# The seam between the LSTM layer and the attention layer: last outputs moved into layer 1's first two steps, its weight loads and first transposes moved ahead

## The chip, the cores and the metric

One core of one Trainium2 chip runs the whole kernel, in fp32. The metric is the device time in microseconds of one execution; the median of three runs stands for a kernel. Beside these runs there is one profiled execution, from which every duration of a single instruction in this text comes.

## The reference

The input x has 128 x 64 tokens of 256 features (8192 tokens), and passes four layers, each of the form x = x + f(relu(layernorm(x))). What matters here is the end of layer 0 and the start of layer 1:

```python
# layer 0: two graph convolutions, then LSTMs over windows of 1 to 4 time steps
h = relu(einsum('ts,bsh->bth', adj, x @ Wg0 + bg0))
h = relu(einsum('ts,bsh->bth', adj, h @ Wg1 + bg1))
for p in range(1, 5):
    nw = T // p
    wins = h[:, :nw * p].reshape(B * nw, p, H)
    last = lstm_last(Wih[p-1], Whh[p-1], bih[p-1], bhh[p-1], wins)
    h = h.at[:, arange(nw) * p + (p - 1)].set(last)
x = x + h
# layer 1: edge attention over 512 edges of a 64-node graph, 4 heads
h  = relu(layernorm(x))
Xq, Xv = h @ W_lin.T, h @ W_val.T
e  = einsum('behd,hd->beh', leaky_relu(Xq[:, src] + Xq[:, dst]), a) + log(A0[src, dst])
x  = x + (segment_softmax(e, src) applied to Xv[:, dst]) @ W_out.T
```

Layer 2 is a graph convolution with batch norms and weights W1 and W2; layer 3 is a dense graph attention.

## The kernel before, in words

**Tiling.** Tokens come in 16 chunks of 512 (NCH), each held as 4 x 128 tokens by 256 features; four chunks make a group (NGR = 4 groups). Matrix products want the features on the partitions, layer norms want the tokens there, so TensorE transposes between the two forms: `transpose_features` (transposes L153, ACT copy L156) turns a normed chunk to features-first; `add_transposed` (transposes L167, DVE add L172) turns an LSTM result back and adds it to the residual.

**End of layer 0.** The LSTMs run as products (L643) of TensorE with Strassen-like quarter sums, and gates: ACT activations L671, DVE additions L697 and L702, the cell update L720 and L721, tanh L724, and the hidden state `hT` L737 (these line numbers are those of the profile of before). Products land in a PSUM pool in which `bank()` has two buffers. A list of slots orders the products; for each group, two calls of `group_out(g, c)` are hung behind the slots. Such a call takes two chunks: for each, 8 transposes, 2 DVE adds into the residual tile `xres` (4 buffers, loaded from x by SP in `fetch_x`, L764), and one store of the new x into `xa[n]` on POOL's queue (L776). The calls of the last group come after the last slot, when there are no products left.

**Start of layer 1.** The first two chunks of `xa` are loaded and normed among the last LSTM slots (`x_first`, `first_norms1`). Then the code allocates layer 1's pools (its PSUM pool gives `bank()` four buffers), issues on SP the loads of the weights `wlv` and `wout`, of layer 2's `w1T` and `w2T`, of six vectors, and of chunks 2 and 3 (`load_x1`, tiles `xin`); it transposes chunk 0, projects two tiles of 128 tokens, and enters the loop over pairs of tiles, `edges(q)`, q = 0 to 31. A step of it gathers queries to the edges (L964), lets ACT copy the result (L970) and DVE apply the leaky relu (L971), scores (L980), projects the next pair (`project`, L948, with copies L954 and L955), and norms chunks ahead: statistics on DVE (L87, L88), roots on POOL (L99 to L102), scaling on ACT (L109). `w1T` gets four POOL instructions of quarter sums (L136). The residual tiles `xo` of layer 1 are loaded from `xa` by SP (L1121).

**What sets the order.** Each engine runs its instructions in order. A planner places them by its own priorities; `late(...)` marks an instruction that keeps its place in program order. A tile pool makes the first writer of a buffer wait for the last users of its memory, and pools opened later reuse the memory of pools that were closed, so a load can wait for layer 0's last readers of that place.

Of the kernel before, what the change touches and what calls it, by code (L numbers as in the profile page):

```python
# [9 lines left out]
F32 = mybir.dt.float32  # L10
# [20 lines left out]
def gnn_stack_kernel(ctx: ExitStack, tc: tile.TileContext, a: dict, out: bass.AP):  # L31
# [373 lines left out]
            yield  # L405


    with ExitStack() as l0:
        w0 = l0.enter_context(tc.tile_pool(name="w0", bufs=1))
        wsp = l0.enter_context(tc.tile_pool(name="wsp", bufs=1))  # L410

        hTs0 = [w0.tile([P, 2, 2, UNIT], F32, tag=f"hT{k}", name=f"hT{k}") for k in range(NGR // 2)]
# [169 lines left out]
        hop = lpool("hop2", 2)  # L582
        cp = lpool("cp", 2)
        gp = lpool("gp", 8)
        xres = lpool("xres", 4)

        class Step:

# [172 lines left out]

        def fetch_x(n):
            xt = xres.tile([P, 4, D], F32, tag="xres", name="xres")
            nc.sync.dma_start(out=xt, in_=token_tiles(a["x"], n))  # L764
            return xt

        residual = {}
# [41 lines left out]
        steps[0].prepare()  # L809
        for slot in range(len(tasks) + 2):  # L810
            new = tasks[slot] if slot < len(tasks) else None
            if new:
                step = steps[new[0]]
                one = step.gate(new[1])
                next(one)
            if len(flight) > 1:
                old = flight.pop(0)
                next(old[1], None)
                next(flight[-1][1])
            elif flight and not new:  # L820
                old = flight.pop(0)
                next(old[1], None)
            else:
                old = None
                if flight:
                    next(flight[-1][1])
            if new:
                next(one)
                flight.append((new, one))
                at, k = new[0], new[2]  # L830
                while outs and outs[0][0] <= slot:
                    group_out(*outs.pop(0)[1:])

                new_half = at + 1 < len(steps) and at and steps[at + 1].w == 1 < step.w
                if k == len(step.gates) - (1 if new_half else 2) and at + 1 < len(steps):
                    steps[at + 1].prepare()
                if step.w == MAX_SKIP and step.t == 2 and k < 2:
                    for u in range(2):
                        n = 4 * step.g + 2 * u + k
                        later.append((slot, "x", n))  # L840
            while later and later[0][0] <= slot:
                _, kind, n = later.pop(0)
                residual[n] = fetch_x(n)
            next(norm_steps, None)
            while later_weights and later_weights[0][0] <= slot:
                _, ph = later_weights.pop(0)
                weights["ih", ph] = Weights("ih", phases[ph])
            if old:
                (at, q, k), step = old[0], steps[old[0][0]]
                if k == len(step.gates) - 1:  # L850
                    if at + 1 == len(steps) or steps[at + 1].phase != step.phase:
                        phase_over(step.phase)
                    if step.phase == len(phases) - 1 and step.t == 1 and step.g == NGR - 1:

                        t_ = wsp.tile([P, 2, 4, 2, P], F32, tag="wih", name="x_first", bufs=2)
                        flat = t_.rearrange("p k q j m -> p k (q j m)")
                        norms1 = {}
                        for n in range(2):
                            xt = flat[:, n, :].rearrange("p (i d) -> p i d", i=4)
                            nc.sync.dma_start(out=xt, in_=token_tiles(xa[n]))  # L860
                            norms1[n] = Norm(xt)
                        norm_steps = first_norms1(norms1)
                    if step.w == MAX_SKIP and step.t == MAX_SKIP - 1:
                        outs += [(slot + 1, step.g, 0), (slot + 2, step.g, 1)]
        for _ in norm_steps:
            pass
        for _, g, c in outs:
            group_out(g, c)
    psums["banks"] = None
    w12 = ctx.enter_context(tc.tile_pool(name="w12", bufs=1, side="right"))  # L870
    xin1 = l01.enter_context(tc.tile_pool(name="xin1", bufs=2, side="right"))

    def load_x1(n, chunks=xa):
        xt = xin1.tile([P, 4, D], F32, tag="xin1", name="xin1")
        nc.sync.dma_start(out=xt, in_=token_tiles(chunks[n]))
        return xt


    with ExitStack() as l1:
# [5 lines left out]
            return l1.enter_context(tc.tile_pool(name=name, bufs=bufs, reuse_waits="tile"))  # L885


        t1 = pool("t1", 2)
        lrp = pool("lrp", 6)
        t3 = pool("t3", 4)  # L890
        w1 = pool("w1", 1)
        vp = pool("vp", 3)
        KEPT = 4
        vk = pool("vk", KEPT)
        yp = pool("yp", 2)
        xo = pool("xo", 4)
        e1 = pool("e1", 1)
        attp = pool("attp", 3)
        attc = pool("attc", 3)
        wlv = w1.tile([P, 2, 2 * D], F32, tag="wlv", name="wlv")  # L900
        nc.sync.dma_start(out=wlv[:, :, :D], in_=a["W_linT"])
        nc.sync.dma_start(out=wlv[:, :, D:], in_=a["W_valT"])
        wout = w1.tile([P, 2, D], F32, tag="wout", name="wout")
        nc.sync.dma_start(out=wout, in_=a["W_outT"])


        w1T = w12.tile([P, 2, 512], F32, tag="w1T", name="w1T")
        nc.sync.dma_start(out=w1T, in_=a["W1T"])
        w2T = w12.tile([P, 4, D], F32, tag="w2T", name="w2T")
        nc.sync.dma_start(out=w2T, in_=a["W2T"])  # L910
        w1S = w12.tile([P, 3, 2, P], F32, tag="w1S", name="w1S")
        w1Q = quarter_sums(w1T.rearrange("p k (q j m) -> p k q j m", q=2, j=2), w1S)
        x_rs = w12.tile([P, NCH, 4], F32, tag="x_rs", name="x_rs")
        x_nm = w12.tile([P, NCH, 4], F32, tag="x_nm", name="x_nm")
        vec = {}
        for name, width in (("b1", 4), ("g1", 4), ("be1", 4), ("b2", 2), ("g2", 2), ("be2", 2)):
            vec[name] = w12.tile([P, width], F32, tag=name, name=name)
            nc.sync.dma_start(out=vec[name], in_=a[name])
        hTs, queries, values, scores, waiting = {}, {}, {}, {}, []

        def sums1(m, tiles):

# [17 lines left out]
        def project(it):  # L940

            n, i = it // 4, it % 4
            if i == 0:
                kept = n >= NCH - KEPT
                values[n] = (vk if kept else vp).tile([P, 4, D], F32, tag="xv", name="xv")
            p = bank()
            for k in range(2):
                ins = nc.tensor.matmul(  # L948
                    p, hTs[n][:, k, i * P : (i + 1) * P], wlv[:, k, :], start=k == 0, stop=k == 1
                )  # L950
                if k == 0:
                    late(ins)
            xq = queries[it] = t3.tile([P, D], F32, tag="xq", name="xq")
            nc.scalar.copy(xq, p[:, :D])  # L954
            (nc.vector.tensor_copy if i % 2 else nc.scalar.copy)(values[n][:, i, :], p[:, D:])  # L955
            if i == 3 and n < NCH - KEPT:
                nc.gpsimd.dma_start(out=xv_mem[n], in_=values.pop(n))
# [147 lines left out]
        def fetch(n):  # L1105
# [4 lines left out]
                xv = vp.tile([P, 4, D], F32, tag="xv", name="xv_in")  # L1110
                nc.sync.dma_start(out=xv, in_=xv_mem[n])
            if n < NCH - 3:
                xt = xo.tile([P, 4, D], F32, tag="xo", name="xo")
            else:

                if n < NCH - 1:
                    t = t1.tile([P, 2, CHUNK], F32, tag="hT1", name="xo_last")
                else:
                    t = w1.tile([P, 2, 2 * D], F32, tag="wlv", name="xo_last")
                xt = t.rearrange("p c t -> p (c t)").rearrange("p (i d) -> p i d", d=D)  # L1120
# [3 lines left out]
        def turn_attention(n):  # L1124

            g, m = n // 4, n % 4
            att = attc.tile([P, 2, 8, T], F32, tag="att", name="att")
            for o in range(2):
                late(
                    (nc.vector.tensor_copy if o else nc.scalar.copy)(  # L1130
# [52 lines left out]
        def sums(n, xt, keep=False):  # L1183
# [3 lines left out]
            for i in range(4):  # L1187
                nc.vector.bn_stats(st[:, i, :], xt[:, i, :])
                nc.vector.bn_aggr(mv[:, i, :], st[:, i, :])
            rs, nm = x_rs[:, n, :], x_nm[:, n, :]  # L1190
            ins = nc.gpsimd.tensor_scalar(rs, mv[:, :, 1], 1e-5, None, ALU.add)
            if keep:
                late(ins)
# [63 lines left out]
        def edges(q):  # L1257
# [5 lines left out]
            for it in tiles:  # L1263
                if it + 2 < NT:
                    project(it + 2)
            if not odd:
                turn1(n + 1)
                sums1(n + 2, (2, 3))
# [15 lines left out]
                    turn_attention(k)  # L1284

        coming1 = {n: load_x1(n) for n in (2, 3)}
        hTs[0] = t1.tile([P, 2, CHUNK], F32, tag="hT1", name="hT1")
        for ip in range(2):
            transpose_features(norms1[0].h, hTs[0], ip)
        sums1(2, (0, 1))  # L1290
        for it in range(2):
            project(it)
        for q in range(NT // 2):
            edges(q)
            last_one = q == NT // 2 - 1

            for _ in range(4 if last_one else 0):
# [8 lines left out]
        def scale_x(n, xt, keep=late):  # L1306

            h2[n] = hpool.tile([P, 4, D], F32, tag="h", name="h")
            for i in range(4):
# [2 lines left out]
                        h2[n][:, i, :],  # L1312
                        xt[:, i, :],
                        AF.Relu,
                        bias=x_nm[:, n, i : i + 1],
                        scale=x_rs[:, n, i : i + 1],
                    )
                )

# [12 lines left out]
        while unnormed:  # L1332
            sums(*unnormed.pop(0))
    l01.close()


    with ExitStack() as l2:
# [623 lines left out]
```

## Time and profile before

| | us |
|---|---|
| median of 3 runs | 2087.89 |
| lowest and highest run | 2086.41, 2092.74 |
| profiled execution | 2079.25 |
| span of the profile | 2077.5 |
| TensorE busy (PE) | 2013.7 (97%) |
| DVE, ACT, POOL busy | 1359.9, 1180.2, 315.7 |
| granted TensorE clock, mean | 0.994 |

PE is TensorE's matmul stream (transposes too), PEld its weight loads, which overlap it. L-numbers are lines of the kernel. An engine's own time within a stretch is read from the windows view, what it waited for from the waits view, the order of one engine's work from its timeline. In a timeline a row is the start, the time from the first to the last of the instructions put together, the engine, line, operation and count, and in brackets the idle time ahead of it and who ended it. SPq and POOLq are the queues on which those engines issue transfers.

### The profile page before, as it was taken

Reading aid. Unit: us, or ns where it says so; the run is one execution under the profiler, and the core shown is the slowest. Engines: PE = TensorE matmul, PEld = TensorE weight load, DVE = VectorE, ACT = ScalarE, POOL = GpSimd, SP = SyncE. Lnnn points to the kernel's source line nnn. Section 1 sums busy time; section 2 is a strip of 40 time slices with the busy share of each in tenths; the row PEclk is TensorE's granted clock in tenths of the full one; section 3 lists DMA queues with packets and bytes.
Section 4 is the critical chain, followed back from the end, with each engine's and each line's share of the span. In section 5 each row is a group of like instructions: output and inputs, shape, how many; then the busy total and the mean of one; then the engine's idle time right before and its main releaser. Section 6 shows DMA issues by size and latency. Waiting matters only on the chain.

```text
span 2077.5 us, 25503 instructions
## 1 busy us (share of the span) xinstructions
PE 2013.7 (97%) x9444; PEld 1350.0 (65%) x9444; DVE 1359.9 (65%) x2508; ACT 1180.2 (57%) x2226; POOL 315.7 (15%) x422
## 2 busy tenths in 40 slices
PE   8999999999999999999999998999999999999998
PEld 6777478866688845886667886333334765434786
DVE  7664666564665567567446555677777767786776
ACT  4344766554555467566456563666675456592444
POOL 3000010110100021002001001223233420000563
PEclk9999999999999999999999999999999999999999
DMA  8421000100100160001001006213234851022012
GB/s 276 134 96 52 0 21 1 41 0 1 41 1 1 64 220 21 1 1 41 1 0 41 1 1 205 74 51 98 76 92 123 253 185 59 0 71 91 31 62 71
DMA packets 94460, 135.06 MB, mean 65 GB/s; under 512 B 6400, under 2 KB 82048, under 8 KB 92160
## 3 DMA queue, kind: packets, MB, share of 16 engines
q1 hardware_dynamic: 87616, 109.11, 16.0%
q0 software_dynamic: 6112, 24.12, 4.0%
q8 instruction: 74, 1.21, 0.2%
q14 instruction: 50, 0.41, 0.1%
q10 hardware_dynamic: 608, 0.20, 0.0%
HBM read 87.28 MB, written 46.14 MB: 64 GB/s over the span
## 4 chain that ended last, share of the span: by engine, by line
PE 87%; DVE 6%; ACT 3%; DMA 2%; issue 1%; POOL 1%; ACTq 0%; POOLq 0%; DVEq 0%; SPq 0%
PE pa L643 25%; PE bank L50 13%; PE pc L643 13%; PE pb L643 6%; PE pair L964 6%; PE bank L948 5%; PE pa L1396 5%; PE bank L980 3%; PE bank L1169 3%; PE pc L1396 2%; PE pb L1396 1%; PE pair L50 1%; ACT gate L671 1%; PE pair L1148 1%; PE bank L167 1%
## 5 line engine op out<-in xcount | busy, mean ns | idle before, releaser
L643 PE MATMUL pa<-xop,sih 128*128 128x256 f32 (+2 forms) x1056 | 344.3, 418 | 10.1 <-DVE gate L697 6.4
L671 ACT ACTIVATE gate<-gate,bias 128x256 f32<-128x256 f32 (+2 forms) x368 | 247.1, 678 | 173.5 <-DVE gate L687 91.2
L643 PEld LDWEIGHTS pa<-xop,sih 128*128 128x128 f32 x1056 | 198.3, 190 | 86.4 <-issue 22.8
L643 PE MATMUL pc<-xop,wih 128*128 128x256 f32 (+2 forms) x736 | 251.1, 423 | 0.0
L687 DVE TENSOR_TENSOR gate<-pb,gate 128x256 f32<-128x256 f32 (+2 forms) x184 | 87.6, 476 | 225.7 <-PE pb L643 154.1
L643 PE MATMUL pa<-lstm_h,shh 128*128 128x256 f32 (+1 forms) x672 | 212.7, 398 | 0.0
L971 DVE SCALAR_TENSOR_TENSOR lr<-lr 128x1024 f32<-128x1024 f32 x128 | 150.5, 1218 | 55.6 <-ACT lr L970 55.6
L643 PEld LDWEIGHTS pc<-xop,wih 128*128 128x128 f32 x736 | 139.8, 190 | 51.2 <-issue 23.0
L702 DVE TENSOR_TENSOR gate<-pc,gate 128x256 f32<-128x256 f32 (+2 forms) x184 | 87.6, 476 | 119.7 <-PE pc L643 119.4
L970 ACT COPY lr<-pair 128x1024 f32<-128x1024 f32 x128 | 123.1, 1014 | 45.1 <-PE pair L964 45.1
L643 PEld LDWEIGHTS pa<-lstm_h,shh 128*128 128x128 f32 x672 | 127.7, 190 | 30.2
L643 PE MATMUL pc<-lstm_h,whh 128*128 128x256 f32 (+1 forms) x448 | 141.8, 398 | 0.0
L686 ACT COPY gate<-pa 128x256 f32<-128x256 f32 (+2 forms) x184 | 76.0, 413 | 96.7 <-PE pa L643 96.4
L964 PE MATMUL pair<-sd_hot,xq 64*128 64x512 f32 x512 | 127.6, 616 | 2.4 <-ACT lr L970 2.3
L948 PE MATMUL bank<-wlv,hT 128*128 128x512 f32 x256 | 118.1, 604 | 0.2 <-ACT hT L156 0.2
L697 DVE TENSOR_TENSOR gate<-pa,gate 128x256 f32<-128x256 f32 (+2 forms) x184 | 87.5, 475 | 44.0 <-PE pa L643 43.4
L691 ACT COPY gate<-pa 128x256 f32<-128x256 f32 (+2 forms) x184 | 75.4, 410 | 59.0 <-PE pa L643 57.7
L671 ACT ACTIVATE gate<-pa,bias 128x256 f32<-128x256 f32 (+2 forms) x184 | 94.0, 511 | 26.1 <-PE pa L643 24.4
L434 POOL TENSOR_TENSOR sih<-wih 128x512 f32<-128x512 f32 x8 | 11.8, 1474 | 624.8 <-DMA wih<-in_WihT 295.9
L643 PE MATMUL pa<-xop,wih 128*128 128x256 f32 (+1 forms) x320 | 101.4, 398 | 2.7 <-ACT xop L624 2.7
L643 PE MATMUL pb<-xop,wih 128*128 128x256 f32 (+1 forms) x320 | 100.3, 398 | 1.6 <-DVE gate L687 1.6
L643 PEld LDWEIGHTS pc<-lstm_h,whh 128*128 128x128 f32 x448 | 85.1, 190 | 20.1
(338 smaller groups left out, 3814.8 us busy)
## 6 DMA issues: line engine op xcount, KB each, us to landing
field<-sd_hot SPq DMA_DIRECT2D x8, 1152.0 KB, 11.4
wih<-in_WihT SPq DMA_DIRECT2D x8, 1024.0 KB, 5.0
xres<-in_x SPq DMA_DIRECT2D x16, 512.0 KB, 4.5
xa<-xres POOLq DMA_DIRECT2D x16, 512.0 KB, 5.3
xin<-xb SPq DMA_DIRECT2D x16, 512.0 KB, 3.9
h<-xb SPq DMA_DIRECT2D x16, 512.0 KB, 3.9
xin<-in_x SPq DMA_DIRECT2D x15, 512.0 KB, 5.5
out_x<-h SPq DMA_DIRECT2D x15, 512.0 KB, 2.9
```

What stands on the lines that cost most here:

```text
L50: nc.tensor.matmul(o, lhsT, rhs, start=start, stop=stop)
L643: ins = nc.tensor.matmul(p[:, : self.N], weights[kind, self.phase](k, q), x[k], start=first_ and kind == "ih", stop=kind == "hh" or not se ...
L671: nc.scalar.activation(out, in_, AF.Tanh if q == 2 else AF.Sigmoid, bias=bias[:, self.w - 1, 2 * q + j : 2 * q + j + 1],)
L686: nc.scalar.copy(blk[0, 0], pa[:, :N])
L687: nc.vector.tensor_tensor(blk[0, 0], pb[:, :N], blk[0, 0], ALU.add)
L697: nc.vector.tensor_tensor(blk[1, 1], pa[:, :N], blk[1, 1], ALU.add)
L702: nc.vector.tensor_tensor(blk[1, 0], pc[:, :N], blk[1, 0], ALU.add)
L948: ins = nc.tensor.matmul(p, hTs[n][:, k, i * P : (i + 1) * P], wlv[:, k, :], start=k == 0, stop=k == 1)
L964: ins = nc.tensor.matmul(p[:, par, :], queries[it][r, c * P : (c + 1) * P], sd_hot[r, :], start=True, stop=True)
L970: nc.scalar.copy(lr, p)
L971: nc.vector.scalar_tensor_tensor(lr, lr, 0.2, lr, ALU.mult, ALU.max)
L1396: ins = nc.tensor.matmul(p, lhs[k], x[k], start=first_, stop=last_one, skip_group_check=True)
```

## The change

1. `group_out` for the last group is no longer called after the LSTM slots. Its two calls are made in `edges(0)` and `edges(1)`, behind the projections. The pool of `xres` and that of the hidden states live until q = 1 is done, on the other side of the memory.
2. `wlv` and `wout` are loaded ahead of the last four loads of x, which move from the slots to layer 1's start and are kept in program order by `late`.
3. The transposes of chunk 0 go to the first slot behind the last LSTM product in the program, into a gate buffer (`first_hT`), in program order.
4. The loads of layer 2's weights and vectors, the quarter sums of `w1T`, and the pools `vk`, `xo` and `attc` come after q = 1 (`layer2_weights`). Other pools of layer 1 change their order of allocation; `xin1` moves to the left side.

```diff
+    l0out = ExitStack()
+    w0 = l0out.enter_context(tc.tile_pool(name="w0", bufs=1, side="right"))
     with ExitStack() as l0:
-        w0 = l0.enter_context(tc.tile_pool(name="w0", bufs=1))
...
-        xres = lpool("xres", 4)
+        xres = l0out.enter_context(
+            tc.tile_pool(name="xres", bufs=4, side="right", reuse_waits="tile")
+        )
...
         def fetch_x(n):
             xt = xres.tile([P, 4, D], F32, tag="xres", name="xres")
-            nc.sync.dma_start(out=xt, in_=token_tiles(a["x"], n))
+            ins = nc.sync.dma_start(out=xt, in_=token_tiles(a["x"], n))
+            if n >= NCH - NCH // 4:
+                late(ins)
             return xt
...
         for slot in range(len(tasks) + 2):
             new = tasks[slot] if slot < len(tasks) else None
+            if slot == len(tasks):
+                for _ in norm_steps:
+                    pass
+                first_hT = gp.tile([P, 4 * NMAX], F32, tag="gate", name="hT1_first")
+                first_hT = first_hT[:, : 2 * CHUNK].rearrange("p (c t) -> p c t", c=2)
+                for ip in range(2):
+                    transpose_features(norms1[0].h, first_hT, ip, late)
...
-                if step.w == MAX_SKIP and step.t == 2 and k < 2:
+                if step.w == MAX_SKIP and step.t == 2 and k < 2 and step.g < NGR - 1:
                     for u in range(2):
                         n = 4 * step.g + 2 * u + k
                         later.append((slot, "x", n))
...
-        for _ in norm_steps:
-            pass
-        for _, g, c in outs:
-            group_out(g, c)
+        last_outs = [(g, c) for _, g, c in outs]
     psums["banks"] = None
-    w12 = ctx.enter_context(tc.tile_pool(name="w12", bufs=1, side="right"))
-    xin1 = l01.enter_context(tc.tile_pool(name="xin1", bufs=2, side="right"))
...
         nc.sync.dma_start(out=wlv[:, :, :D], in_=a["W_linT"])
         nc.sync.dma_start(out=wlv[:, :, D:], in_=a["W_valT"])
         wout = w1.tile([P, 2, D], F32, tag="wout", name="wout")
         nc.sync.dma_start(out=wout, in_=a["W_outT"])
-        w1T = w12.tile([P, 2, 512], F32, tag="w1T", name="w1T")
-        nc.sync.dma_start(out=w1T, in_=a["W1T"])
...
+        for g, c in last_outs:
+            for u in range(2):
+                n = 4 * g + 2 * u + c
+                residual[n] = fetch_x(n)
...
+        def layer2_weights():
+            w12 = ctx.enter_context(tc.tile_pool(name="w12", bufs=1, side="right"))
+            w1T = w12.tile([P, 2, 512], F32, tag="w1T", name="w1T")
+            nc.sync.dma_start(out=w1T, in_=a["W1T"])
...
+            w1S = w12.tile([P, 3, 2, P], F32, tag="w1S", name="w1S")
+            w1Q = quarter_sums(w1T.rearrange("p k (q j m) -> p k q j m", q=2, j=2), w1S)
...
             for it in tiles:
                 if it + 2 < NT:
                     project(it + 2)
+            if last_outs:
+                group_out(*last_outs.pop(0))
             if not odd:
                 turn1(n + 1)
                 sums1(n + 2, (2, 3))
...
         coming1 = {n: load_x1(n) for n in (2, 3)}
-        hTs[0] = t1.tile([P, 2, CHUNK], F32, tag="hT1", name="hT1")
-        for ip in range(2):
-            transpose_features(norms1[0].h, hTs[0], ip)
+        hTs[0] = first_hT
         sums1(2, (0, 1))
         for it in range(2):
             project(it)
         for q in range(NT // 2):
             edges(q)
+            if q == 1:
+                l0out.close()
+                layer2_weights()
+                for name, bufs in (("vk", KEPT), ("xo", 4), ("attc", 3)):
+                    later_pools[name] = pool(name, bufs)
```

More of the change, by code (lines that the diff above doesn't have):

```diff
@@ L864, in gnn_stack_kernel @@
                         outs += [(slot + 1, step.g, 0), (slot + 2, step.g, 1)]
-        for _ in norm_steps:
-            pass
-        for _, g, c in outs:
-            group_out(g, c)
+        last_outs = [(g, c) for _, g, c in outs]
     psums["banks"] = None
-    w12 = ctx.enter_context(tc.tile_pool(name="w12", bufs=1, side="right"))
-    xin1 = l01.enter_context(tc.tile_pool(name="xin1", bufs=2, side="right"))
[L873 to L876, printed above, removed]
     with ExitStack() as l1:
@@ L885, in pool, with load_x1 @@
             return l1.enter_context(tc.tile_pool(name=name, bufs=bufs, reuse_waits="tile"))
+        KEPT = 4
+        w1 = pool("w1", 1)
         t1 = pool("t1", 2)
+        t3 = pool("t3", 4)
+        vp = pool("vp", 3)
         lrp = pool("lrp", 6)
[L890 to L894, printed above, removed]
+        xin1 = pool("xin1", 2)
         yp = pool("yp", 2)
-        xo = pool("xo", 4)
         e1 = pool("e1", 1)
         attp = pool("attp", 3)
-        attc = pool("attc", 3)
+        later_pools = {}
+        def load_x1(n, chunks=xa):
+            xt = xin1.tile([P, 4, D], F32, tag="xin1", name="xin1")
+            nc.sync.dma_start(out=xt, in_=token_tiles(chunks[n]))
+            return xt
         wlv = w1.tile([P, 2, 2 * D], F32, tag="wlv", name="wlv")
@@ L904, in gnn_stack_kernel @@
         nc.sync.dma_start(out=wout, in_=a["W_outT"])
-        w1T = w12.tile([P, 2, 512], F32, tag="w1T", name="w1T")
[L908 to L918, printed above, removed]
-        hTs, queries, values, scores, waiting = {}, {}, {}, {}, []
+        for g, c in last_outs:
+            for u in range(2):
+                n = 4 * g + 2 * u + c
+                residual[n] = fetch_x(n)
+        hTs, queries, values, scores, waiting = {}, {}, {}, {}, []
+        vec, w12t = {}, {}
+        def layer2_weights():
+            w12 = ctx.enter_context(tc.tile_pool(name="w12", bufs=1, side="right"))
+            w1T = w12.tile([P, 2, 512], F32, tag="w1T", name="w1T")
+            nc.sync.dma_start(out=w1T, in_=a["W1T"])
+            w2T = w12.tile([P, 4, D], F32, tag="w2T", name="w2T")
+            nc.sync.dma_start(out=w2T, in_=a["W2T"])
+            w1S = w12.tile([P, 3, 2, P], F32, tag="w1S", name="w1S")
+            w1Q = quarter_sums(w1T.rearrange("p k (q j m) -> p k q j m", q=2, j=2), w1S)
+            x_rs = w12.tile([P, NCH, 4], F32, tag="x_rs", name="x_rs")
+            x_nm = w12.tile([P, NCH, 4], F32, tag="x_nm", name="x_nm")
+            for name, width in (("b1", 4), ("g1", 4), ("be1", 4), ("b2", 2), ("g2", 2), ("be2", 2)):
+                vec[name] = w12.tile([P, width], F32, tag=name, name=name)
+                nc.sync.dma_start(out=vec[name], in_=a[name])
+            w12t.update(w1T=w1T, w2T=w2T, w1Q=w1Q, x_rs=x_rs, x_nm=x_nm)
         def sums1(m, tiles):
@@ L944, in project @@
                 kept = n >= NCH - KEPT
-                values[n] = (vk if kept else vp).tile([P, 4, D], F32, tag="xv", name="xv")
+                values[n] = (later_pools["vk"] if kept else vp).tile([P, 4, D], F32, tag="xv", name="xv")
             p = bank()
@@ L1112, in fetch @@
             if n < NCH - 3:
-                xt = xo.tile([P, 4, D], F32, tag="xo", name="xo")
+                xt = later_pools["xo"].tile([P, 4, D], F32, tag="xo", name="xo")
             else:
@@ L1126, in turn_attention @@
             g, m = n // 4, n % 4
-            att = attc.tile([P, 2, 8, T], F32, tag="att", name="att")
+            att = later_pools["attc"].tile([P, 2, 8, T], F32, tag="att", name="att")
             for o in range(2):
@@ L1189, in sums @@
                 nc.vector.bn_aggr(mv[:, i, :], st[:, i, :])
-            rs, nm = x_rs[:, n, :], x_nm[:, n, :]
+            rs, nm = w12t["x_rs"][:, n, :], w12t["x_nm"][:, n, :]
             ins = nc.gpsimd.tensor_scalar(rs, mv[:, :, 1], 1e-5, None, ALU.add)
@@ L1314, in scale_x @@
                         AF.Relu,
-                        bias=x_nm[:, n, i : i + 1],
-                        scale=x_rs[:, n, i : i + 1],
+                        bias=w12t["x_nm"][:, n, i : i + 1],
+                        scale=w12t["x_rs"][:, n, i : i + 1],
                     )
@@ L1334, in gnn_stack_kernel @@
     l01.close()
+    w1T, w2T, w1Q, x_rs, x_nm = (w12t[k] for k in ("w1T", "w2T", "w1Q", "x_rs", "x_nm"))
     with ExitStack() as l2:
```

## The prediction

> **What bounds the kernel now.** I read the busy lines of the page first: TensorE does 97% of the span, so what can be won is the 3% in which it waits, and what the edit can win lies where it waits between the last LSTM product and the steady part of layer 1.
>
> ```profile
> span 2077.5 us, 25503 instructions
> PE 2013.7 (97%) x9444; PEld 1350.0 (65%) x9444; DVE 1359.9 (65%) x2508; ACT 1180.2 (57%) x2226; POOL 315.7 (15%) x422
> ```
>
> The windows view then compares that passage (1267.59, where L643 resumes after the transposes of group 2, to 1309.06, the first gather of pair q=2) with the 39 us behind it. Columns: stretch, length, busy us of PE, PEld, DVE, ACT, POOL, granted clock, DMA share, GB/s.
>
> ```profile
> 1267.59:1309.06 41.47, 34.06 (x149) 17.45 (x147) 21.46 (x34) 17.38 (x30) 11.70 (x15) 0.96 0.72 236
> 1309.06:1348.00 38.94, 38.94 (x176) 14.71 (x176) 24.59 (x37) 25.52 (x41) 7.53 (x10) 1.00 0.16 55
> ```
>
> Layer 1 proper keeps PE busy all the time; the passage idles 7.41 us, and its 34.06 are partly slow. The PE timeline (start, us, work, idle before it) and the waits view (waiter <- releaser: total, times, longest) say where:
>
> ```profile
> 1277.02 6.51 PE L167 MATMUL bank<-ident,hT 128*128 128x128 f32 x32 [4.26 <-DVE hT L737]
> 1284.64 3.70 PE L948 MATMUL bank<-wlv,hT 128*128 128x512 f32 x8 [0.24 <-ACT hT L156]
> 1309.06 2.04 PE L964 MATMUL pair<-sd_hot,xq 64*128 64x512 f32 x8 [2.03 <-ACT lr L970]
> ```
>
> ```profile
> DVE ln_st L87 <- DMA xin<-xa: 4.9, 1, 4.9
> PE bank L167 <- DVE hT L737: 4.3, 1, 4.3
> PE pair L964 <- ACT lr L970: 2.0, 1, 2.0
> ```
>
> Three losses. (1) After the last product PE stands 4.26 us until tanh, gate and hT (L724, L671, L737) are through. (2) The 32 transposes then take 6.51 us, against 32 x 0.1125 = 3.6 at full speed: each two-bank turn waits for a DVE add of 0.70. (3) The 2.03 at the end: the chain of waits leads back through L970 behind L109 on ACT, the roots on POOL, the statistics on DVE, to a load issued late on SP (SP's timeline, and the chain's line for that load):
>
> ```profile
> 1291.70 0.35 SPq L908 DMA_DIRECT2D w1T<-in_W1T  x1
> ...
> 1294.94 0.43 SPq L918 DMA_DIRECT2D be<-in_be  x1
> 1295.46 1.66 SPq L875 DMA_DIRECT2D xin<-xa  x2
> ```
>
> ```profile
> 1295.46 4.06 DMA xin<-xa
> ```
>
> xin of chunk 2 goes out at 1295.46 only because w1T in front of it waited to 1291.70 for layer 0's last stores.
>
> **What the Trainium skill says.** "DMA: Bandwidth & Descriptors", section "Anatomy of one DMA — SWDGE (gpsimd) path": DMA engines do not wait on semaphores; the issuing sequencer does. So whatever stands behind a waiting issue waits too. The SP queue agrees: wlv, needing only its own buffer, goes out at 1272.89, right after the fourth x load (1272.4), which waited for a store. "TensorE: Matmul & The Clock Gate", section "What's actually happening": after an idle window (about 3.4 us) the clock is halved. Here the 4.26 us gap is followed by a granted clock of 0.69 in 1275–1280 and 0.97 in 1280–1285. "Perfetto Trace Analysis", section "Matmuls": independent groups should rotate through PSUM banks so that their evacuation overlaps. The LSTM's two banks show what too few cost (loss 2); layer 1 has four.
>
> **The change part by part.** The instruction order of each engine is taken from the two built programs.
>
> *PE.* Nothing is removed: L167 x32, L153 x16, three L948 groups of 8, four L964 groups of 8, L980 x24 stay. From the gather of q=2 on, order and index are the same. PE work at full speed in the passage: LSTM tail 2.60 + 1.73, L167 3.6, L153 16 x 0.11 = 1.8, L948 3 x 3.63 = 10.9, L964 4 x 1.92 = 7.7, L980 0.93 + 1.85 = 2.8: 31.1. So 10.4 of 41.47 is loss. I walk the new order from 1267.59.
>
> - The 8 transposes L153 of chunk 0 now stand ahead of the last ten LSTM products. They need banks freed by the third and fourth add of group 2 (DVE, to 1267.76 and 1268.36): 0.9 of work and 0.3 of waiting, L643 resumes at 1268.8. The 0.59 us wait for L697 stays. Last product done at 1272.76 + 1.2 = 1274.0. Their two ACT copies (0.54 each) precede gate activations that wait for these products anyway: nothing.
> - Then, instead of the 4.26 gap: L948 of tiles 0 and 1 (to 1277.6; its input first_hT and wlv are long there), L964 (1279.5), L948 of tiles 2 and 3 (1283.1). L964 needs xq copied by ACT, which is busy with L724 and L671 to about 1276.3; the copies fall ahead of 1277.6.
> - 16 transposes L167 need hT (about 1278.3; they start at 1283.1: covered), 8 L153 follow: 1.8 + 0.9, plus 0.3 for DVE adds in the four-bank rotation: 1286.1.
> - L964 1288.0, L980 1289.0, L964 1290.9, L948 1294.5, 16 L167 with 0.25 of waiting 1296.6, L964 1298.5, L980 1300.3.
>
> The gather of q=2 starts at 1300.3 against 1309.06: **8.8 us earlier**; of the 10.4, about 1.6 remain.
>
> *DVE.* The eight adds (5.6) now fall in q=0 and q=1, behind the xv copies, no longer one after another with PE waiting. From 1274 to 1300 DVE then has these adds, six leaky steps L971 (7.1), statistics (1.9) and three xv copies (1.3): 16 us in 26. Two statistics of xin(2) stand in front of the xv copy and adds of q=0, so the load must land by about 1282.
>
> *SP.* wlv (two) and wout pass the four x loads; they wait only for the readers of x_first and go out near 1206, far ahead of need. The x loads keep their times (1262.18 to 1272.4), being held by the same stores. xin(2), xin(3) follow, held by the last LSTM product using xop: 1273.5 to 1274.6. Landing 4.3 us median in this stretch: 1278–1279, three before need. w1T, w2T and the six vectors now wait for the last L167 (1296.3); w1T lands near 1301. The four xo loads move behind xa13 and xa15; their reader, the residual of layer 1, comes much later: nothing.
>
> *POOL.* The last stores move later by 5 to 12 us. w1T's sums (4 x 0.73) stand ahead of xv1's store and the roots of xin(3), and end near 1304; those roots wait for DVE till about 1307.5: nothing, with four us of cover.
>
> *ACT.* Only positions change. L109 for chunk 2 needs the roots near 1292.3 (statistics 1288, four POOL steps 4.3), stands at 1294.5: loss (3) goes.
>
> *Between layers 1 and 2* three loads of x2 now stand behind a store's wait on SP, out at 1679.4 to 1680.4 instead of 1671.8 to 1679; landing 7.9 median there: 1687.3 to 1688.3, first needed 1689.55. Bounds: 0 to 1 us lost (11.2, the longest load of the window above). I take 0.
>
> Sum: 8.8 us. Upper bound 10.4 (the whole loss); lower bound from the rivals. Against the profiled execution, 2079.25 us (1.75 outside its span), that is 2070.4. The median shown, 2087.89, lies 8.6 us (0.4%) above that execution; the saving is taken off it: 2079.1.
>
> **The rivals.**
>
> *Half of it comes back.* With adds inside q=0 and q=1, in-order DVE, or the bank rotation, paces PE: each of the eight adds costs its 0.70 on the path, up to 5.6. For: 32 transposes took 6.51 for exactly this reason. Against: four banks, and 16 us of DVE work in 26. Gain 3.2 to 6: 2082 to 2085, around the limit of what counts.
>
> *Slower.* xin(2) stands behind four x loads that wait for stores, and DVE's statistics of it stand in front of everything PE needs in q=0. If that load lands late, DVE, the adds, banks and PE stop. Every us beyond 1282 is lost: at 1291 the gain is gone, at 1297 it is 0.3% slower. A store or load of 18.5 us, the longest load from xa in the run, would put issue at 1288, landing at 1295, and the time at about 2092. Against: stores from xa took 3.9 here, and the x loads show 1272.4 as the last.
>
> *It does not do what it says.* The scheduler could have left the transposes; the built order shows them moved. Excluded for the order; a wait that I place wrongly in it belongs to the first rival.
>
> **How the numbers follow.** 0.3% (6.3 us) is about what a measurement of this kernel can tell from no change. First case, gain 7 to 11, time 2077 to 2081: 0.73. Half back, 2082 to 2086: 0.2, nearly all within 0.3%. Slower: 0.07, of which 0.01 still ends within the bound. So faster 0.73, same 0.21, slower 0.06. Range 2075 to 2086: the first case with 2 us of scatter between runs (the runs before lie 1.5 below and 4.9 above their median), and most of the second; the slow case is left out.
>
> **What would show it.** Right: no wait of L167 for L737, L948 straight after L643, clock near 1.00 through 1275–1285, 32 L167 in two groups of about 2 us, xin issued near 1274 and its DVE wait gone, the q=2 gather near 1300. Wrong: DVE waiting for xin at L87 near 1282, PE waiting at L167 or L153 for L172 by more than 1 us in sum, waits on x2 loads near 1690, or a span less than 6 us shorter.

## The result, and the profile after

| | before | after |
|---|---|---|
| median of 5 runs each (the first three of before have the same median) | 2087.89 us | 2077.85 us |
| lowest and highest run | 2086.41, 2092.74 | 2075.05, 2079.75 |
| profiled execution, span | 2079.25, 2077.5 | 2077.24, 2075.4 |

The ratio of the runs is 0.9948, with a 95% interval of 0.9933 to 0.9963: faster by 8 to 14 us. The forecast was 2079.1 us and 8.8 us saved. Two further measurements of the same pair, below, give 0.9955 and 0.9960.

One thing in the table looks wrong: the spans differ by 2.1 us only, and a span less than 6 us shorter was among the prediction's signs of being wrong. The profiled execution of before (2079.25) is none of its five runs and lies 7 us under the lowest of them, while that of after is one of its five. So it most likely comes from another chip, one on which before takes about 2080 us. The record names no chip for this table; what speaks for it stands under before_look, further down. The passage itself is not touched by it.

This is the PE timeline of the changed kernel through the passage (start, us, work, idle before it). L647, L966, L982 and L998 are the lines L643, L948, L964 and L980 of before.

```profile
1266.13 1.25 PE L153 MATMUL bank<-ident,h 128*128 128x128 f32 x8 [0.19 <-DVE xres L172]
1267.22 0.60 PE L647 MATMUL pa<-xop,sih 128*128 128x256 f32 x2
...
1270.57 0.70 PE L647 MATMUL pa<-xop,sih 128*128 128x256 f32 x2 [0.59 <-DVE gate L701]
...
1272.40 3.60 PE L966 MATMUL bank<-wlv,hT_first 128*128 128x512 f32 x8
1275.92 1.99 PE L982 MATMUL pair<-sd_hot,xq 64*128 64x512 f32 x8
1277.84 3.70 PE L966 MATMUL bank<-wlv,hT_first 128*128 128x512 f32 x8
1281.38 1.91 PE L167 MATMUL bank<-ident,hT 128*128 128x128 f32 x16
1283.13 1.19 PE L153 MATMUL bank<-ident,h 128*128 128x128 f32 x8
...
1292.61 2.40 PE L167 MATMUL bank<-ident,hT 128*128 128x128 f32 x16
...
1298.71 1.99 PE L982 MATMUL pair<-sd_hot,xq 64*128 64x512 f32 x8
```

Layer 1 begins in the instant in which the last product ends; the 4.26 us for hT are gone, and the 32 transposes take two groups of 1.91 and 2.40 us, not 6.51. The windows view says the same of the stretch that was 41.47 us long, and of the 10 us in which the clock had dropped to 0.69 and 0.97 (columns as before):

```profile
1265.95:1298.71 32.76, 31.89 (x148) 16.56 (x149) 22.85 (x35) 18.26 (x30) 7.47 (x11) 1.00 0.52 165
1275.00:1280.00 5.00, 5.00 (x16) 1.91 (x15) 3.78 (x4) 2.63 (x5) 0.00 (x0) 1.00 0.53 178
1280.00:1285.00 5.00, 5.00 (x32) 3.53 (x32) 4.60 (x11) 2.05 (x5) 1.33 (x2) 1.00 0.24 99
```

The waits view of PE over this passage holds two entries; the waits for L737 and for L970 are not among them, and DVE has no wait for xin. SP's timeline shows why: xin goes out at 1272, not 1295.

```profile
PE pa L647 <- DVE gate L701: 0.6, 1, 0.6
PE bank L153 <- DVE xres L172: 0.2, 1, 0.2
```

```profile
1226.14 0.56 SPq L911 DMA_DIRECT2D wlv<-in_W_linT  x1
...
1260.55 10.68 SPq L768 DMA_DIRECT2D xres<-in_x  x4
1272.16 1.41 SPq L907 DMA_DIRECT2D xin<-xa  x2
1295.04 0.34 SPq L927 DMA_DIRECT2D w1T<-in_W1T  x1
```

### The profile page after: what moved, and what is told of

It is laid out like the page before. It is cut to its first block, busy times and chain, and to the rows that moved or that the text cites. A ratio compares the mean times of both kernels' runs of the same rounds, so it can differ in the third digit from the quotient of the medians.

```text
span 2075.4 us, 25506 instructions
## 1 busy us (share of the span) xinstructions
PE 2016.3 (97%) x9444; PEld 1353.5 (65%) x9444; DVE 1359.9 (66%) x2508; ACT 1180.0 (57%) x2226; POOL 312.3 (15%) x422
## 5 line engine op out<-in xcount | busy, mean ns | idle before, releaser
L647 PE MATMUL pa<-xop,sih 128*128 128x256 f32 (+2 forms) x1056 | 344.2, 418 | 10.9 <-DVE gate L701 7.1
L647 PEld LDWEIGHTS pa<-xop,sih 128*128 128x128 f32 x1056 | 198.2, 190 | 87.5 <-issue 22.8
L647 PE MATMUL pc<-xop,wih 128*128 128x256 f32 (+2 forms) x736 | 251.1, 423 | 0.0
L647 PE MATMUL pa<-lstm_h,shh 128*128 128x256 f32 (+1 forms) x672 | 212.7, 398 | 0.0
L647 PEld LDWEIGHTS pc<-xop,wih 128*128 128x128 f32 x736 | 139.8, 190 | 51.2 <-issue 23.0
L647 PEld LDWEIGHTS pa<-lstm_h,shh 128*128 128x128 f32 x672 | 127.7, 190 | 30.2
L647 PE MATMUL pc<-lstm_h,whh 128*128 128x256 f32 (+1 forms) x448 | 141.8, 398 | 0.0
L982 PE MATMUL pair<-sd_hot,xq 64*128 64x512 f32 x512 | 127.5, 616 | 0.3 <-ACT lr L988 0.3
L701 DVE TENSOR_TENSOR gate<-pa,gate 128x256 f32<-128x256 f32 (+2 forms) x184 | 87.6, 476 | 44.0 <-PE pa L647 43.4
L966 PE MATMUL bank<-wlv,hT 128*128 128x512 f32 x240 | 110.7, 604 | 0.0
L647 PE MATMUL pa<-xop,wih 128*128 128x256 f32 (+1 forms) x320 | 101.4, 398 | 2.7 <-ACT xop L628 2.7
L647 PE MATMUL pb<-xop,wih 128*128 128x256 f32 (+1 forms) x320 | 100.3, 398 | 0.4 <-DVE gate L691 0.4
L647 PEld LDWEIGHTS pc<-lstm_h,whh 128*128 128x128 f32 x448 | 85.1, 190 | 20.1
```

Of the source, the lines that this page charges most:

```text
L647: ins = nc.tensor.matmul(p[:, : self.N], weights[kind, self.phase](k, q), x[k], start=first_ and kind == "ih", stop=kind == "hh" or not se ...
L701: nc.vector.tensor_tensor(blk[1, 1], pa[:, :N], blk[1, 1], ALU.add)
L966: ins = nc.tensor.matmul(p, hTs[n][:, k, i * P : (i + 1) * P], wlv[:, k, :], start=k == 0, stop=k == 1)
L982: ins = nc.tensor.matmul(p[:, par, :], queries[it][r, c * P : (c + 1) * P], sd_hot[r, :], start=True, stop=True)
```

## The experiments

The two PE streams are paired matmul by matmul; the **passage** of a kernel is by how much its lead over before grows from 1265 to 1318 us. It is free of what happens elsewhere. The changed kernel has 8.76 in each of its three traces. The runs fell on different chips: on one the runs of before have a median of 2079.67 us (outs_back, transposes_back, wlv_act_late, xin_early), on the others 2086.38 (after_again, mid, part4_alone, both_q0) and 2085.95 (before_look, after_third, mid_again, transposes_again). So a ratio is taken to before on the same chip, and the microseconds in the expectations of the first four, which assumed the slower chip, are read as differences.

| kernel | passage, us shorter than before | ratio to before, 95% interval |
|---|---|---|
| changed kernel, again | 8.76 | 0.9955 (0.9942 to 0.9969) |
| changed kernel, third time | 8.76 | 0.9960 (0.9947 to 0.9974) |
| outs_back | 3.35 | 0.9989 (0.9983 to 0.9996) |
| transposes_back | 7.30 | 0.9962 (0.9948 to 0.9975) |
| transposes_again | 7.31 | 0.9965 (0.9951 to 0.9979) |
| wlv_act_late | -1.81 | 1.0002 (0.9994 to 1.0010) |
| xin_early | -4.50 | one run |
| part4_alone | 0.50 | 0.9997 (0.9989 to 1.0006) |
| both_q0 | 6.95 | 0.9960 (0.9945 to 0.9976) |
| mid | 10.18 | 0.9958 (0.9944 to 0.9971) |
| mid_again | 10.18 | 0.9948 (0.9935 to 0.9962) |

Each measured interval contains the ratio that the passage alone gives (8.76 of 2086 is 0.9958, 3.35 of 2080 is 0.9984, 7.31 of 2086 is 0.9965). In every trace the lead made in the passage then stays as it is up to 1575 us, within 0.02 us. Behind that, single traces drift apart, most of all in the gaps described under before_look, and also by 0.9 us ahead to 4.5 us behind from 1640 us to the end (before_look 0.8 ahead, the three traces of the changed kernel 0.2 to 0.5 behind). So the gain is made in the passage; a difference of a microsecond or two that a kernel makes far behind it is not resolved here.

**outs_back: the last outputs ahead of layer 1 again.**

```diff
+        while last_outs:
+            group_out(*last_outs.pop(0))
         coming1 = {n: load_x1(n) for n in (2, 3)}
```

> The changed kernel, but both last calls of group_out are made ahead of layer 1's first projection; weights and first transposes stay where the change put them. Theory (the gain is work put under the tail of the LSTM gates): PE ends its last product near 1272.4, waits about 4.3 us for hT, then its 32 transposes follow the eight DVE adds (8 x 0.62 = 5.0 us, against 4.3 for the two groups of 16 in the changed kernel), and L966 starts near 1282 instead of 1272.4, with 4.3 us of transposes already done: 5 to 7.5 us more than the changed kernel, 2083 to 2085.5 us. Rival (the gain comes from elsewhere: the memory layout, other waits, clock spells in later layers): within 2 us of the changed kernel, 2076 to 2080.

The passage loses 5.4 of the 8.76. PE's timeline has the gap back, 4.17 us, and the transposes are slow again:

```profile
1275.96 5.37 PE L167 MATMUL bank<-ident,hT 128*128 128x128 f32 x32 [4.17 <-DVE hT L741]
```

The theory holds in its sum; the rival of a gain made elsewhere falls. But the reason given for the slow transposes, the row of adds, is only part of it: the clock is at 0.66 from 1275 to 1280, behind the gap (the third number from the end), and in both_q0 below the same 32 in a row on four banks, without a gap ahead of them, took 4.13 us.

```profile
1275.00:1280.00 5.00, 4.04 (x22) 4.04 (x23) 3.35 (x5) 0.00 (x0) 0.75 (x1) 0.66 0.38 122
```

Of the 3.35 us that stay, the 2.03 for L970 are the larger part: that wait is gone here too. The rest is mostly in the transposes (5.37 us against 6.51).

**transposes_back, transposes_again: chunk 0's transposes behind the last product.**

```diff
-                first_hT = gp.tile([P, 4 * NMAX], F32, tag="gate", name="hT1_first")
-                first_hT = first_hT[:, : 2 * CHUNK].rearrange("p (c t) -> p c t", c=2)
-                for ip in range(2):
-                    transpose_features(norms1[0].h, first_hT, ip, late)
...
-        hTs[0] = first_hT
+        hTs[0] = t1.tile([P, 2, CHUNK], F32, tag="hT1", name="hT1")
+        for ip in range(2):
+            transpose_features(norms1[0].h, hTs[0], ip)
```

> The changed kernel, but chunk 0's transposes stand behind the last product, and land in a buffer of t1, as before. Theory: the last product ends 1.1 us earlier (near 1271.3), the transposes take 0.9, but their ACT copies stand behind tanh and the last sigmoid (L728, L675, to about 1273.6), so L966 starts near 1274.1 instead of 1272.4: 1.7 us more, about 2079.6 us. Rival (these transposes carry most of the gain, since without them layer 1 cannot start under the gates): the copies keep PE idle [...], 4 us or more.

> transposes_back once more, on one chip with the changed kernel. Theory: its passage is 1.5 us longer than the changed kernel's, its median 1 to 2 us higher. Rival: the same median or a lower one.

The passage loses 1.46 us. The first projection waits, as reckoned, for ACT, which has to finish tanh and the last sigmoid before it copies; this pause of 1.75 us did not lower the clock (1.00 in 1275 to 1285):

```profile
1274.33 3.70 PE L962 MATMUL bank<-wlv,hT 128*128 128x512 f32 x8 [1.75 <-ACT hT L156]
```

On one chip its median (2079.62) lies 0.95 us above the changed kernel's, just under the 1 to 2 us expected; the intervals do not separate the two, the traces do. So this part carries a sixth of the gain.

**wlv_act_late: the weights late again.**

```diff
-        nc.sync.dma_start(out=wlv[:, :, :D], in_=a["W_linT"])
-        nc.sync.dma_start(out=wlv[:, :, D:], in_=a["W_valT"])
+        late(nc.scalar.dma_start(out=wlv[:, :, :D], in_=a["W_linT"]))
+        late(nc.scalar.dma_start(out=wlv[:, :, D:], in_=a["W_valT"]))
```

> The changed kernel, but the two loads of wlv are issued by ACT, in program order, behind the last sigmoid (about 1274.6) instead of by SP near 1226; in the kernel before they went out at 1272.9 and 1273.5. Theory: PE's first L966 needs wlv; issue 1274.6 plus 5.7 us (the landing before) is 1280.3, against 1272.4: 8 us more, and a little more by the clock after such a gap, 2085 to 2088 us, so without the early weights the whole gain is gone. Rival (PE's order or the queues let it run on, or the load lands in 4 us): 5.5 us or less, under 2083.5.

They went out at 1273.97 and 1274.63, just ahead of the last sigmoid (1274.66) and not behind it, and took 6.3 us each. PE stood for 7.85 us, and then ran its first projections at half speed (clock 0.50 in 1280 to 1285; 6.16 us against 3.60):

```profile
1281.11 6.16 PE L966 MATMUL bank<-wlv,hT_first 128*128 128x512 f32 x8 [7.85 <-DMA wlv<-in_W_valT]
```

7.85 and some 2.5 for the clock are the 10.6 us that the passage loses against the changed kernel: more than the whole gain. Without the early load the rest of the change is worse than before. That an early load alone would bring nothing is argued, not run: in the kernel before wlv had landed by 1279.3, and its first use, at 1284.64, waited for hT.

**xin_early: in the kernel before, only the loads of chunks 2 and 3 ahead of w1T's.**

```diff
         nc.sync.dma_start(out=wout, in_=a["W_outT"])
+        coming1 = {n: load_x1(n) for n in (2, 3)}
...
-        coming1 = {n: load_x1(n) for n in (2, 3)}
```

> The kernel before, with one edit: the loads of chunks 2 and 3 for layer 1 are issued ahead of w1T's. Theory: they still wait for the last stores of layer 0, whose buffers lie in the same memory, so they go out near 1291.7 instead of 1295.46; POOL's roots stand behind the quarter sums of w1T, which end near 1300, so the roots start about 1 us earlier than 1301.5 and PE's wait of 2.03 us ahead of the gather of q=2 shrinks to about 1. Rival (the load is all that was late): the wait of 2.03 us disappears.

Both sides were wrong: the passage got 4.5 us longer, and PE's wait grew from 2.03 to 3.32 us. xin went out at 1291.06, early as expected. But w1T, now behind it, landed 6.4 us after its issue (3.7 in the kernel before), and the quarter sums on POOL, ahead of the roots, took more than twice as long (first the kernel before, then xin_early):

```profile
1295.57 0.72 POOL L136 TENSOR_TENSOR w1S<-w1T 128x256 f32<-128x256 f32 x1 [10.26 <-DMA w1T<-in_W1T]
```

```profile
1298.63 1.73 POOL L136 TENSOR_TENSOR w1S<-w1T 128x256 f32<-128x256 f32 x1 [13.88 <-DMA w1T<-in_W1T]
1300.44 1.58 POOL L136 TENSOR_TENSOR w1S<-w1S,w1T 128x256 f32<-128x256 f32 x1
1301.99 1.70 POOL L136 TENSOR_TENSOR w1T<-w1T 128x256 f32<-128x256 f32 x1
1303.65 1.71 POOL L136 TENSOR_TENSOR w1S<-w1T,w1S 128x256 f32<-128x256 f32 x1
```

In that time DVE ran four leaky steps, which took 6.18 us where four took 4.60 in the kernel before (again first before, then xin_early):

```profile
1301.32 4.60 DVE L971 SCALAR_TENSOR_TENSOR lr<-lr 128x1024 f32<-128x1024 f32 x4
```

```profile
1298.58 6.18 DVE L972 SCALAR_TENSOR_TENSOR lr<-lr 128x1024 f32<-128x1024 f32 x4
```

The Trainium skill, "SBUF — State Buffer", section "SBUF: two separate sides", says that DVE and GpSimd (POOL) share a pair of ports, which whichever starts first holds for its whole instruction, when the DVE instruction has two SBUF inputs and the GpSimd one reads SBUF. The traces agree. In all fourteen together 22 leaky steps begin while one of these sums runs: 21 of them take 1.74 to 1.76 us, one that begins 0.15 us before the sum's end takes 1.23, and every other step takes 1.19 to 1.28. In the trace of after, the third sum, begun 0.06 us ahead of such a step, keeps its 0.73 us; the fourth, begun in the middle of that step, takes 1.71. While DVE was idle, in the kernel before, each sum took 0.72 to 0.73. The roots ended at 1307.9 where they had ended near 1306.0, and this trace runs 1.0 us ahead of that of before.

The longer wait is 1.3 of the 4.5 us. About 1.2 are lost in the first scores (2.25 us for 1.06), for the reason shown under part4_alone; 1.6 in the gather and the projection behind the wait, at a clock of 0.69 from 1310 to 1315; and 0.4 in the transposes, where the old gap of 4.25 us was followed by a clock of 0.50, not 0.69.

**part4_alone: the kernel before, with w1T's load behind those of chunks 2 and 3 and the quarter sums behind the roots of chunk 2.**

```diff
-            nc.gpsimd.tensor_tensor(o, x, y, op)
+            ins = nc.gpsimd.tensor_tensor(o, x, y, op)
+            if keep:
+                keep(ins)
...
+        def layer2_weights():
+            nc.sync.dma_start(out=w1T, in_=a["W1T"])
...
+            w1Qs.append(quarter_sums(w1T.rearrange("p k (q j m) -> p k q j m", q=2, j=2), w1S, late))
...
             edges(q)
+            if q == 1:
+                layer2_weights()
...
```

> The kernel before, with the loads of chunks 2 and 3 ahead of w1T's and the quarter sums of w1T behind the roots of chunk 2 on POOL. Theory (in xin_early the roots were late only because they stood behind quarter sums, slowed by DVE): xin goes out near 1291 as in xin_early, statistics end near 1298.6, the roots near 1301.5, scaling on ACT is done when L970 needs it, PE's wait of 2.03 is gone: 2 us less than before in the passage. Rival (the roots are slowed by DVE all the same, or the load lands late): the wait is at least 1 us, or larger than before.

The wait for L970 is gone, so in xin_early the POOL queue was its cause (in the kernel before, the sums had ended by 1298.5 and the roots waited for xin until 1301.5). But the passage gains 0.5, not 2.0: a new wait stands in PE's timeline, and DVE's shows where it comes from.

```profile
1294.90 1.04 PE L985 MATMUL bank<-lr,afield 128*32 128x512 f32 x2
1296.61 1.06 PE L985 MATMUL bank<-lr,afield 128*32 128x512 f32 x6 [0.66 <-DVE lr L976]
```

```profile
1288.79 1.23 DVE L976 SCALAR_TENSOR_TENSOR lr<-lr 128x1024 f32<-128x1024 f32 x1 [1.22 <-ACT lr L975]
1294.47 0.43 DVE L87 BATCH_NORM_STATS2 ln_st<-xin 128x6 f32<-128x256 f32 x1 [4.46 <-DMA xin<-xa]
...
1295.34 1.21 DVE L976 SCALAR_TENSOR_TENSOR lr<-lr 128x1024 f32<-128x1024 f32 x1
```

DVE waits 4.46 us for xin in the middle of a pair of leaky steps, and the second is what the score needs: the eight products of that score take 2.7 us from the first to the next gather (1.0 in the kernel before), which eats 1.7 of the 2.03. That is the "slower" rival of the prediction in small: statistics of a late load ahead of work that PE waits for. Reordering the loads does not help here, because they still wait for layer 0's stores (to 1290); the changed kernel's xin does not wait for those, and goes out 18 us earlier.

**both_q0: both last calls in q = 0.**

```diff
-            if last_outs:
+            while last_outs:
                 group_out(*last_outs.pop(0))
```

> The changed kernel, but both last calls of group_out stand in q=0. Theory (four banks hide the adds): the eight adds in a row take 8 x 0.62 = 5.0 us against 3.6 of transposes, so PE waits 1 to 1.5 us more for banks in q=0 and 0.5 less in q=1: 0.5 to 1 us more than the changed kernel. Rival (adds in layer 1's steps pace PE): 3 us more or worse.

The passage is 1.8 us worse than the changed kernel's, more than the 0.5 to 1 us expected and for another reason. The adds cost little: 32 transposes in a row took 4.13 us, against 1.91 and 2.40. The loss is at the gather of q=2, again through POOL: w1T goes out at 1288.05, when the last of the 32 transposes ends, its sums move in among the roots of chunk 2, ACT scales late.

```profile
1302.98 2.04 PE L982 MATMUL pair<-sd_hot,xq 64*128 64x512 f32 x8 [1.53 <-ACT lr L988]
```

**mid, mid_again: chunk 0's transposes one slot later.**

```diff
-            if slot == len(tasks):
+            if slot == len(tasks) + 1:
```

> The changed kernel, but chunk 0's eight transposes stand one slot later, between the sixth and the seventh of the last ten LSTM products, where PE waits 0.59 us for L701. Theory: their 0.9 us fill that wait, and the wait of 0.19 for the second bank goes too, so L966 starts 0.6 to 0.8 us earlier than in the changed kernel: the best kernel so far by that much, which a median hardly shows. Rival: their ACT copies (2 x 0.58) now stand between the gates, hT comes later, and nothing is gained or up to 1 us is lost.

> mid once more. Theory: its passage is 1.4 us shorter than the changed kernel's, as in its first trace, and its median lies 1 to 2 us lower than that of after_third. Rival: within 0.7 us of it, the 1.4 being given back later.

The passage gets 1.42 us shorter than the changed kernel's, in both traces. The eight transposes now fill the pause for L701, so that they cost almost nothing:

```profile
1268.47 1.04 PE L153 MATMUL bank<-ident,h 128*128 128x128 f32 x8
1269.34 0.60 PE L647 MATMUL pa<-xop,sih 128*128 128x256 f32 x2
```

In the changed kernel they cost 1.44 us ahead of the products, and the pause stayed. So the gain is about twice the 0.6 to 0.8 us expected: the whole 1.44 goes, not only the waits. The medians were 1.56 and 1.44 us below the changed kernel's on the same chips, but the intervals overlap; both are clear of before. By its passage it is the best version here.

**after_again, after_third, before_look: the same pair on other chips.**

> The changed kernel once more, beside the kernel before on the same chip. Theory (the whole gain is the passage between the last LSTM products and layer 1): the first gather of q=2 comes 8.7 us earlier than before, and the median lies 8 to 10 us under that of before, while transposes_back (7.2 us earlier in its passage) and outs_back (about 3) keep their order. Rival (the 10 us of the first measurement were partly chip and chance): 6 us or less.

> The changed kernel beside mid_again and transposes_again on one chip. Theory: 8 to 10 us under before, passage 8.7 us. Rival: under 6 us.

> The kernel before once more, for its profile. Theory (the median of before lay 8.6 us above its profiled execution because the two came from different chips; on one of them 64x64 products near 1580 to 1590 are fed slowly, whatever the kernel): if this chip is the one whose runs of before lie near 2087, gaps at those products and a half clock behind them show here too, 5 to 7 us lost there; if its runs lie near 2080, none. Rival (the gaps come from the change): none in either case.

The changed kernel was 8.16 and 7.28 us below before (medians 2078.22 and 2078.67); the second falls short of the 8 to 10 us expected, while its passage came as expected. In before_look the passage is that of the first trace (0.19 us apart), but between 1588 and 1598 it loses 5.4 us against it, in the products of 64 x 64 and behind them:

```profile
1588.35 1.32 PE L1148 MATMUL pair<-att,xv_in 64*64 64x64 f32 x44
1590.06 0.35 PE L1148 MATMUL pair<-att,xv_in 64*64 64x64 f32 x4 [0.40 <-issue]
1590.81 0.35 PE L1148 MATMUL pair<-att,xv_in 64*64 64x64 f32 x5 [0.39 <-issue]
...
1593.07 5.27 PE L1169 MATMUL bank<-wout,yT 128*128 128x256 f32 x16 [0.41 <-issue]
```

In the first trace of before the same 64 products took 1.16 us in one piece and the 16 behind them 3.72. All eight traces from chips on which before takes 2086 have these gaps, the changed kernel's too; of the four traces from the chip with 2080 none has them at this place. So the change does not cause them. They do not cost every kernel the same: 5.4 us in before_look, 6.1 to 6.6 in the three traces of the changed kernel. On such chips up to about 1 us of the passage is given back here, which fits the 8.16 and 7.28. Why some chips feed these products slowly, and why the cost differs, is open.

## Why the prediction was right

The main case held, in time (2077.85 for 2079.1) and step by step. That the time came so close is in part chance: its interval is 8 to 14 us of gain, and the other two pairs of medians gave 8.2 and 7.3. The steps are the stronger evidence. The trace of after runs 1.64 us ahead of that of before already at the transposes of group 2; with that added, its times stand beside the walk:

| step | predicted | measured |
|---|---|---|
| last product done | 1274.0 | 1274.04 |
| projections of tiles 2 and 3 done | 1283.1 | 1283.02 |
| first 16 transposes and chunk 1's done | 1286.1 | 1285.88 |
| projections of tiles 4 and 5 done | 1294.5 | 1294.25 |
| gather of q=2 starts | 1300.3 | 1300.35 |

- **PE:** 8.76 us for 8.8. The bank waits ahead of chunk 0's transposes were there (1.44 us in all for 1.2).
- **DVE:** the adds took 2.48 us per four. The first group of 16 transposes kept its pace (1.91 us), the second lost about half a microsecond (2.40) where 0.25 was put down; the "half comes back" rival is out. Even the eight in a row of both_q0 held the transposes up by no more than half a microsecond (4.13 against 3.6).
- **SP:** the load of xin went out at 1273.8 in before's clock, as worked out (1273.5), and DVE never waited for it; the "slower" rival did not arise. (In its sum for a store of 18.5 us, an issue at 1288 and the 4.3 us of landing make 1292.3, not the 1295 given.) wlv left at 1226, not near 1206 as the prediction had it; the 46 us to its use make that harmless.
- **POOL:** the roots took 2.9 us instead of 4.3. w1T's sums ended at 1304.9 in before's clock, near the 1304 worked out, though the last took 1.71 where 0.73 was put down, beside a leaky step on DVE.
- **Layers 1 and 2:** no wait on a load of x2 appears near 1690.

What was mis-sized is not in the passage. The 8.6 us between the profiled execution and the median of before were taken as an offset that both kernels share. They are, as far as the runs show, the difference of two chips, much of it in the 64 x 64 products: in the trace of after these cost 6.1 us that they did not cost in that of before. So the 2070.4 us given for a profiled execution could not be compared with the 2077.24 that came, and the span, named as a sign of being wrong, misled. Against the median the sum was right because both of them, by the same signs, come from one chip. Loss 2, too, was put down to the two banks alone. Set beside outs_back (5.37 us, four banks, behind a gap) and both_q0 (4.13, four banks, no gap), the 6.51 us of before are, by an estimate from these three times, about 1.2 us of clock and 1.1 of banks over 4.13; with the gap gone both went, so the sum did not suffer. And the split into three losses was not additive, as xin_early and part4_alone show: the 2.03 us at the gather could not be had alone by the earlier issue tried there, because the roots stood behind w1T's sums and the leaky steps behind xin's statistics.

## What to carry to other kernels

A tail of gate arithmetic in which TensorE has nothing to do is filled by the next stage's first products, provided that everything which they need, weights above all, has landed before the tail: a late weight load cost more than the whole gain. Walk the new order instruction by instruction from one profile, with the wait of each; here that gave the gain to 0.1 us. Moving one load up a queue without looking at what stands behind it on the engines that follow can cost more than the wait that it was to remove.

## What the runs showed of the hardware

- Chips differ on one and the same kernel: 2079.67 against about 2086 us for before, of which 5 to 7 us are lost in gaps of about 0.4 us between small products and the lower clock behind them (0.91 over 1580 to 1600 in before_look, 0.83 in after, 1.00 in the first trace of before). A profile and a median are to be compared only when they come from one chip.
- DVE steps with two inputs and POOL sums of 128 x 256 on SBUF held each other up: 0.73 to about 1.7 us for a sum, 1.22 to 1.74 for a leaky step that began during one. The steps that began during POOL's small root instructions (128 x 4) kept their 1.2 us.
- Pauses of 1.75 us (transposes_back) and 2.03 us (before) on TensorE left the clock at 1.00; one of 3.32 us (xin_early) was followed by 0.69 over 1310 to 1315, and those of 4.17 us (outs_back) and 7.85 us (wlv_act_late) by 0.66 and 0.50. The same pause does not always cost the same: 4.26 us in before and 4.25 us in xin_early were followed by 0.69 and 0.50 over 1275 to 1280.
